# A four-layer hybrid on one core: the pacing estimate of TensorE, and where the first expert's products stand

## The chip, the core and the metric

The kernel runs on one core of a Trainium2 chip. The core has four compute engines, each with an instruction stream of its own that is worked off in order: TensorE (PE in the profile; its weight loads are PEld), VectorE (DVE), ScalarE (ACT) and GpSimd (POOL). SyncE (SP) issues the DMA transfers. The metric is the device time of one execution in microseconds, as a median over runs.

## What is computed

Four images of 32x32 positions (1024 tokens, 256 channels) go through four layers. Cut to what matters:

```python
# layer 0: norm, x @ w_in, 3x3 depthwise conv, gelu; then a selective scan with 512 channels, 64 states
dA = jnp.exp(dtt[:, :, None] * A)
h = dA * h + (dtt * xt)[:, :, None] * Bt[:, None, :]      # one step per token
y = jnp.einsum('bdn,bn->bd', h, Ct)
# layer 1: 1x1 conv, grouped 3x3 conv, 1x1 conv, relu
# layer 2: masked attention (8 heads of 32), then a mixture of 8 experts, hidden size 256
probs = softmax(tokens @ router_w.T); rw, re = top_k(probs, 2); rw = rw / rw.sum()
for e in range(8):
    h = gelu(tokens @ w1[e] + b1[e]); y = h @ w2[e] + b2[e]
    out = out + combine[:, e:e+1] * y
# layer 3: gated selective scan with 512 channels, 16 states; then 8 experts, hidden size 512
```

Each layer's output is added to its input or passed on. Every image needs, in this order: layer 0's front, the layer-0 scan, layers 1 and 2 and layer 3's front, the layer-3 scan, layer 3's end. The images don't depend on each other.

## The kernel before

**Scans.** A scan works in units of 128 rows (channels times states) by 1024 tokens: 256 units for an image in layer 0, 64 in layer 3, 1280 in all, in the order `SCANS` (L31): layer 0 of images 0 and 1, layer 3 of image 0, layer 0 of image 2, layer 3 of image 1, layer 0 of image 3, layer 3 of images 2 and 3. In the numbering of units used below, layer 3's scans begin at units 512, 832, 1152 and 1216. `scans` (L356) issues for each unit: a DMA that spreads the step sizes (`dA`), ScalarE's Exp, two bf16 products of 512 columns (`ps_rep`, L445), VectorE's multiply, VectorE's scan (`h`), GpSimd's multiply, and for every two units four fp32 products into 32 partitions each (`ps_y`, `pair`, L460).

**Side work.** Everything else is written as generators that yield between small steps. `STAGES` (L33) lists them: `front` (layer 0's start) of four images, `middle` (L1786: `back0`, `layer1`, `attention`, `moe(2)`, `front3`) of four, `last` (L1796: `back3`, `moe(3)`, store) of four. A `middle` may begin when its image's layer-0 scan is well on its way, a `last` likewise with layer 3. `advance` (L530) takes one step of the running stage, or chooses the next.

**The order.** Instructions of all engines go out in the order in which the Python code runs; no scheduler changes it. `run` (L552) interleaves by a clock per engine. A wrapper, `Metered`, adds an estimate in microseconds to the issuing engine's clock at every instruction; for TensorE the estimate is `matmul_us` (L71). Twice in each scan unit `run` does:

```python
now = clock["vector"]
for e in clock:
    clock[e] = max(clock[e], now - LAG)
for _ in range(TICKS):
    if max(clock.values()) > clock["vector"] + LEAD or self.advance() is None:
        break
```

So side work is handed out, at most two steps at a time, while no engine's clock is ahead of VectorE's. When all scan units are out, what is left of the stages follows without scans beside it.

**The forced path.** Five units before a scan whose inputs a side stage has not yet issued, `need` (L517) calls `advance` until they are, with no scan unit in between, and sets all clocks equal. `self.alone` then lets attention use the scan's PSUM banks (`ps_sx` for `ps_sc`).

**Attention.** `heads` (L1320) runs, for each of 8 blocks of 128 keys and each pair of heads, four fp32 and bf16 products into scores (`ps_sc`), two more bf16 ones for the mask, ScalarE's Exp, and four fp32 products into 32 partitions each (`ps_at`): 10 products a block, 640 an image.

**Experts.** `moe` (L1442) normalizes and transposes the tokens, makes the router's logits (`ps_lg`), then the routing: a chain of small VectorE operations (`route`, L1569), the transposes of the weights (`ps_ct`), the products with the second bias (`ps_b2`). After that the experts: a pipe of items, of which `one` issues TensorE's part, `two` the Gelu (`h_m`, ScalarE) or the weighted sum into `tb` (VectorE). An item "h" is 128 hidden channels of 512 tokens (two fp32 products of 512 columns, `ps_h`); an item "o" is 256 tokens of output (`ps_e`, fp32, 256 columns). `KH` is 2 in layer 2 and 4 in layer 3.

**Layer 3's front.** `front3` (L1624) makes `ps_p3` and `ps_g3`, the 512x512 product `ps_c3`, the states' inputs `ps_x3`, and in `steps` (L581) the step sizes `ps_dt` and their parts, which the scan needs.

Nearly every instruction goes through the wrapper, so the profile puts it on L124; groups are told apart by the names of their tiles. The profile leaves out digits that end a name (`ps_p` for `ps_p3`).

Of the kernel before, what the change touches and what calls it, by code (L numbers as in the profile page):

```python
# [7 lines left out]
F32 = mybir.dt.float32  # L8
BF16 = mybir.dt.bfloat16
I32 = mybir.dt.int32  # L10
AF = mybir.ActivationFunctionType
ALU = mybir.AluOpType
# [4 lines left out]
P = 128  # L17
NB = 4
L = 1024
TB = L // P  # L20
C = 256
# [3 lines left out]
NEXP = 8  # L25
# [38 lines left out]
def columns(x):  # L64
    n = 1
    for k in x.shape[1:]:
        n *= k
    return n


def matmul_us(out, lhsT=None, rhs=None, **_):  # L71
    if lhsT is None:
        lhsT = out
    us = 0.46e-3 * columns(out)
    if lhsT.dtype != BF16:
        us = max(4 * us, 0.3)
    if out.shape[0] <= 32:
        return us / 4
    return us / 2 if lhsT.shape[0] <= 32 else us


def by_columns(per, fixed, of=0):
# [9 lines left out]
class Metered:  # L92


    COST = {
        "tensor": {"matmul": matmul_us, "transpose": lambda out, *_: 0.3},
        "vector": {
            "tensor_tensor": by_columns(1.18, 0.06), "scalar_tensor_tensor": by_columns(1.5, 0.06),
# [34 lines left out]
class Hybrid:  # L133
# [1308 lines left out]
    def moe(self, which, b, tb):  # L1442

        nc, tc, a = self.nc, self.tc, self.a
        w1, w2, b1, hidden = (
            (a["L2_ffn_w1"], a["L2_ffn_w2"], self.vec["L2_ffn_b1"], 256) if which == 2
            else (a["L3_ffn_W1"], a["L3_ffn_W2"], self.vec["L3_ffn_b1"], 512)
        )
        KH = hidden // P
        with tc.tile_pool(name=f"m{which}{b}", bufs=1, side="right") as op:  # L1450
            xT = op.tile([P, 2, L], F32, name="xTm")
            cw = op.tile([P, TB, NEXP], F32, name="cw")

            def expert_weights(e):
                we1 = op.tile([P, 2, hidden], F32, tag="we1", name="we1", bufs=2)
                nc.sync.dma_start(we1, w1[e].rearrange("(k p) n -> p k n", p=P))
                we2 = op.tile([P, KH, C], F32, tag="we2", name="we2", bufs=2)
                nc.sync.dma_start(we2, w2[e].rearrange("(k p) n -> p k n", p=P))
                return we1, we2

            weights = {0: expert_weights(0)}
            with tc.tile_pool(name=f"mg{which}{b}", bufs=1, side="right") as gp:
                xn = gp.tile([P, TB, C], F32, name="xnm")
                yield from self.norm(gp, tb, TB, xn, "lnm")
                yield from self.turned(xn, TB, xT)
                lg = gp.tile([P, TB, NEXP], F32, name="lg")
                ps = self.ps("ps_lg", (P, TB, NEXP))
                for j in range(TB):
                    for k in range(2):
                        nc.tensor.matmul(  # L1470
                            ps[:, j, :], lhsT=xT[:, k, j * P : (j + 1) * P],
                            rhs=self.router[which][:, k, :], start=(k == 0), stop=(k == 1),
                        )
                yield 3.0
                if which == 2:
                    nc.vector.tensor_copy(lg, ps)
                else:
                    nc.vector.tensor_tensor(
                        lg, ps, self.gb.unsqueeze(1).to_broadcast([P, TB, NEXP]), ALU.add
                    )  # L1480
                yield 0.5
                if which == 2:
                    for j in range(0, TB, 2):
                        tj = tb[:, j : j + 2, :]
                        nc.gpsimd.tensor_tensor(tj, tj, xn[:, j : j + 2, :], ALU.add)
                        yield 0.6
                yield from self.route(gp, lg, cw, which == 2)

                cT = gp.tile([NEXP, L], F32, name="cT")

                def turn(g):
                    ps = self.ps("ps_ct")
                    for k in range(4):
                        nc.tensor.transpose(
                            ps[:NEXP, k * P : (k + 1) * P], cw[:, 4 * g + k, :], self.ident
                        )
                    nc.scalar.copy(cT[:, g * 512 : (g + 1) * 512], ps[:NEXP, :])

                yield from self.pipe(range(2), turn, cost=0.8)
                got = {}  # L1500

                def last(j):
                    got[j] = ps = self.ps("ps_b2", (P, 2, C))
                    for i in range(2):
                        m = 2 * j + i
                        nc.tensor.matmul(
                            ps[:, i, :], lhsT=cT[:, m * P : (m + 1) * P], rhs=self.b2[which],
                            start=True, stop=True,
                        )

                def add(j):
                    tj = tb[:, 2 * j : 2 * j + 2, :]
                    nc.vector.tensor_tensor(tj, got.pop(j), tj, ALU.add)

                yield from self.pipe(range(TB // 2), last, add, cost=1.0)

            hidden_of = {}
            got = {}

            def one(item):  # L1520
                kind, e, g, i = item
                we1, we2 = weights[e]
                if kind == "h":
                    if i == 0:
                        hidden_of[e, g] = op.tile([P, KH, 512], F32, tag="h", name="h_m", bufs=2)
                        if g == 1 and e + 1 < NEXP:
                            weights[e + 1] = expert_weights(e + 1)
                    got[item] = ps = self.ps("ps_h")
                    self.mm(
                        ps, lambda k: we1[:, k, i * P : (i + 1) * P], xT, 2,  # L1530
                        slice(g * 512, (g + 1) * 512),
                    )
                    return
                h = hidden_of[e, g]
                got[item] = ps = self.ps("ps_e", (P, 2, C))
                for s in range(2):
                    m = 2 * i + s
                    for f in range(KH):
                        nc.tensor.matmul(
                            ps[:, s, :], lhsT=h[:, f, m * P : (m + 1) * P], rhs=we2[:, f, :],  # L1540
                            start=(f == 0), stop=(f == KH - 1),
                        )

            def two(item):
                kind, e, g, i = item
                if kind == "h":
                    nc.scalar.activation(
                        hidden_of[e, g][:, i, :], got.pop(item), AF.Gelu,
                        bias=b1[:, e * KH + i : e * KH + i + 1],
                    )  # L1550
                    return
                ps = got.pop(item)
                for s in range(2):
                    m = 4 * g + 2 * i + s
                    nc.vector.scalar_tensor_tensor(
                        tb[:, m, :], ps[:, s, :], cw[:, m, e : e + 1], tb[:, m, :],
                        ALU.mult, ALU.add,
                    )

            items = []  # L1560
            blocks = [(e, g) for e in range(NEXP) for g in range(2)]
            for n in range(len(blocks) + 1):
                if n < len(blocks):
                    items += [("h", *blocks[n], i) for i in range(KH)]
                if n:
                    items += [("o", *blocks[n - 1], i) for i in range(2)]
            yield from self.pipe(items, one, two, cost=2.6 if which == 2 else 3.4)

    def route(self, gp, lg, cw, renorm):  # L1569

# [277 lines left out]
```

## Time and profile before

| | |
|---|---|
| median of 3 runs | 6643.48 us (6634.54 to 6644.86) |
| the profiled execution, its own time | 6636.95 us |
| its span, first to last instruction | 6635.2 us |
| TensorE busy / VectorE / GpSimd / ScalarE | 5360.8 / 5224.0 / 3653.8 / 3439.4 us |
| first scan begins, last scan ends | 204.4 us, 6196.8 us |
| longest stretch between two scans | 5494.2 to 5906.4 us (units 1211 and 1212) |
| mean granted clock of TensorE | 0.829 |

How to read it: the slices cut the span into 40 equal parts and give busy shares in tenths; the clock row is the granted TensorE clock in tenths. A group of instructions is told with its count, its busy time (overlaps counted once) and the mean of one. An fp32 product stands in the trace as two records, so counts of `x16` are eight products; the mean of a record includes its overlap with its neighbours. The rows that matter for what follows:

```profile
L124 POOL TENSOR_TENSOR h<-h,rows 128x1024 f32<-128x1024 f32 x1280 | 3033.0, 2372 | 1900.9 <-DVE h L124 1698.8
L124 DVE TENSOR_TENSOR_SCAN h<-dA,ps_rep 128x1024 f32<-128x1024 f32 x1280 | 2924.0, 2284 | 164.9 <-issue 25.2
L124 DVE TENSOR_TENSOR ps_rep<-ps_rep,rows 128x1024 f32<-128x1024 f32 x1280 | 1552.8, 1213 | 247.7 <-PE ps_rep L124 247.4
L124 PE MATMUL ps_rep<-S,spread_L_conv_A_log 96*128 96x512 bf16 x2048 | 767.5, 465 | 702.5 <-DVE h L124 674.3
L124 PE MATMUL ps_y<-h,collect_L_conv_A_log 128*32 128x512 f32 x4096 | 808.4, 767 | 77.5 <-POOL h L124 76.5
L124 PE MATMUL ps_h<-xTm,we 128*128 128x512 f32 x1536 | 718.9, 608 | 1.4 <-DVE tb L124 1.4
L124 PE MATMUL ps_e<-we,h_m 128*128 128x256 f32 x3072 | 699.6, 381 | 2.3 <-ACT h_m L124 2.3
```

### The profile page before, as it was taken

The page shows a single profiled execution, that of the slowest core. Times are in us where ns is not written, and L with a number is a line of the kernel's source. Part 1 is how long each engine was busy: PE and PEld are TensorE (multiplying, and loading weights), DVE is VectorE, ACT ScalarE, POOL GpSimd, SP SyncE. Part 2 cuts the span into 40 slices and gives each one's busy share as a digit, 9 for nine tenths or more (in the row PEclk, how much of TensorE's full clock was granted, in tenths as well). Part 3 has the DMA queues.
Part 4 walks back from the last instruction along what each step waited for, and adds up shares of the span by engine and source line. Part 5 has one row for each costly group of instructions (what it writes and reads, how often), then busy time and mean ns, then how long its engine had stood idle before and what let it go on. Part 6 is the DMA issues. An engine that isn't in the chain of part 4 may idle for free. (4 is left out here: it accounts for less than half of the span.)

```text
span 6635.2 us, 60077 instructions
## 1 busy us (share of the span) xinstructions
PE 5360.8 (81%) x20320; PEld 2159.1 (33%) x20320; DVE 5224.0 (79%) x4489; ACT 3439.4 (52%) x4114; POOL 3653.8 (55%) x1801
## 2 busy tenths in 40 slices
PE   6568778679798577979789779898699679878979
PEld 3003213122253022234235332243245222524656
DVE  8788998988798997789889997798999972248411
ACT  3426666445477334557658544477478344245411
POOL 0876786755557765555766665556856651045200
PEclk8558779589799568979879789989699789887989
DMA  2444554643245566335555664344644750146221
GB/s 74 151 153 157 182 171 163 190 139 124 101 153 170 190 168 155 112 116 172 175 165 168 189 166 133 105 139 169 200 154 161 196 148 21 45 131 169 74 64 35
DMA packets 348112, 936.90 MB, mean 141 GB/s; under 512 B 37140, under 2 KB 119648, under 8 KB 346144
## 3 DMA queue, kind: packets, MB, share of 16 engines
q1 hardware_dynamic: 345616, 930.35, 44.9%
q8 instruction: 172, 2.82, 0.2%
q0 software_dynamic: 2128, 2.13, 0.2%
q14 instruction: 196, 1.61, 0.1%
HBM read 842.59 MB, written 93.95 MB: 141 GB/s over the span
## 5 line engine op out<-in xcount | busy, mean ns | idle before, releaser
L124 POOL TENSOR_TENSOR h<-h,rows 128x1024 f32<-128x1024 f32 x1280 | 3033.0, 2372 | 1900.9 <-DVE h L124 1698.8
L124 DVE TENSOR_TENSOR_SCAN h<-dA,ps_rep 128x1024 f32<-128x1024 f32 x1280 | 2924.0, 2284 | 164.9 <-issue 25.2
L124 DVE TENSOR_TENSOR ps_rep<-ps_rep,rows 128x1024 f32<-128x1024 f32 x1280 | 1552.8, 1213 | 247.7 <-PE ps_rep L124 247.4
L124 ACT ACTIVATE dA<-dA,A_L_conv_A_log 128x1024 f32<-128x1024 f32 x1024 | 1148.6, 1145 | 609.6 <-DMA dA<-dt 528.6
L124 PE MATMUL ps_rep<-S,spread_L_conv_A_log 96*128 96x512 bf16 x2048 | 767.5, 465 | 702.5 <-DVE h L124 674.3
L124 PE MATMUL ps_y<-h,collect_L_conv_A_log 128*32 128x512 f32 x4096 | 808.4, 767 | 77.5 <-POOL h L124 76.5
L124 PE MATMUL ps_h<-xTm,we 128*128 128x512 f32 x1536 | 718.9, 608 | 1.4 <-DVE tb L124 1.4
L124 PE MATMUL ps_e<-we,h_m 128*128 128x256 f32 x3072 | 699.6, 381 | 2.3 <-ACT h_m L124 2.3
L124 ACT ACT_TABLE_LOAD x497 | 637.7, 1283 | 74.7 <-PE ps_h L124 41.7
L124 PEld LDWEIGHTS <-spread_L_conv_A_log 96*128 96x128 bf16 x2048 | 161.4, 103 | 1485.8 <-DVE h L124 1174.6
L124 PEld LDWEIGHTS ps_e<-we,h_m 128*128 128x128 f32 x3072 | 580.8, 190 | 146.8 <-issue 47.2
L124 DVE SCALAR_TENSOR_TENSOR tb<-ps_e,cw,tb 128x256 f32<-128x256 f32 x512 | 220.8, 474 | 411.1 <-PE ps_e L124 410.8
L124 ACT ACTIVATE h_m<-ps_h,cols 128x512 f32<-128x512 f32 x384 | 260.5, 687 | 485.9 <-PE ps_h L124 483.1
L124 ACT ACTIVATE p<-ps_sc 128x512 f32<-128x512 f32 x432 | 234.4, 594 | 474.7 <-PE ps_sc L124 464.8
L124 PEld LDWEIGHTS ps_h<-xTm,we 128*128 128x128 f32 x1536 | 292.9, 194 | 338.5 <-issue 294.0
L124 ACT ACTIVATE dA<-dA,A_L_attn_A_log 128x1024 f32<-128x1024 f32 x256 | 290.2, 1146 | 189.5 <-DMA dA<-dt 166.0
L124 PE MATMUL ps_at<-p,v 128*32 128x512 f32 x1024 | 354.8, 610 | 39.1 <-ACT p L124 28.2
L124 PE MATMUL ps_rep<-S,spread_L_attn_A_log 96*128 96x512 bf16 x512 | 184.9, 449 | 174.2 <-DVE h L124 163.3
L124 PE MATMUL ps_sc<-qT,kT 32*128 32x512 f32 x864 | 251.3, 653 | 30.1 <-issue 30.1
L124 PE MATMUL ps_at<-p,ones 128*32 128x512 f32 x1024 | 271.9, 610 | 0.0
L124 PEld LDWEIGHTS ps_y<-h,collect_L_conv_A_log 128*32 128x32 f32 x4096 | 107.6, 120 | 474.7 <-POOL h L124 226.9
L124 PE MATMUL ps_cv<-pad,diag 128*128 128x512 f32 x576 | 260.4, 594 | 0.0
(313 smaller groups left out, 5027.7 us busy)
## 6 DMA issues: line engine op xcount, KB each, us to landing
dA<-dt SPq DMA_DIRECT2D x1280, 512.0 KB
we<-in_L_ffn_W_dram SPq DMA_DIRECT2D x64, 512.0 KB
parts<-parts SPq DMA_DIRECT2D x64, 384.0 KB
S<-parts SPq DMA_DIRECT2D x96, 256.0 KB
dt<-sp_r SPq DMA_DIRECT2D x64, 256.0 KB
y<-yo SPq DMA_DIRECT2D x128, 128.0 KB
y_back<-y SPq DMA_DIRECT2D x64, 256.0 KB
we<-in_L_ffn_w_dram SPq DMA_DIRECT2D x64, 256.0 KB
```

Source lines behind the costliest of these rows:

```text
L124: return got(*args, **kw)
```

## The change

Two edits. First, `matmul_us` is written anew. The estimate of a product by its operands, before and after:

| product | before, us | after, us |
|---|---|---|
| bf16, 512 columns, more than 32 rows of weights (`ps_rep`, mask) | 0.236 | 0.369 |
| bf16, 512 columns, 32 rows | 0.118 | 0.230 |
| fp32, 512 columns, into 32 partitions or fewer (`ps_y`, `ps_at`) | 0.236 | 0.440 |
| fp32, 512 columns, 32 rows of weights (scores) | 0.471 | 0.653 |
| fp32, 512 columns, 128 rows (`ps_h`, convolutions) | 0.942 | 0.730 |
| fp32, 256 columns, 128 rows (`ps_e`) | 0.471 | 0.410 |
| fp32, 8 columns (`ps_lg`) | 0.300 | 0.400 |

Second, in `moe` the routing becomes a generator, and the pipe of expert items is made before it runs. After each of the routing's steps one step of the expert pipe is taken, up to 2 x KH of them (which are all "h" items, the first expert's hidden layer); the rest of the pipe runs after the routing. The functions inside (`turn`, `last`, `add`, `one`, `two`) only move. No instruction of the computation is added or removed; loads of ScalarE's tables, which are put in where needed, depend on the order.

```diff
 def matmul_us(out, lhsT=None, rhs=None, **_):
     if lhsT is None:
         lhsT = out
-    us = 0.46e-3 * columns(out)
-    if lhsT.dtype != BF16:
-        us = max(4 * us, 0.3)
-    if out.shape[0] <= 32:
-        return us / 4
-    return us / 2 if lhsT.shape[0] <= 32 else us
+    n = columns(out)
+    few = lhsT.shape[0] <= 32
+    if lhsT.dtype == BF16:
+        return (0.45e-3 if few else 0.72e-3) * n
+    if out.shape[0] <= 32 and n > 32:
+        return 0.86e-3 * n
+    return max(0.09 + (1.1e-3 if few else 1.25e-3) * n, 0.4)
...
-                yield 3.0
-                if which == 2:
+                def routing():
+                    yield 3.0
+                    if which == 2:
...
-                yield from self.route(gp, lg, cw, which == 2)
+                    yield from self.route(gp, lg, cw, which == 2)
...
-            yield from self.pipe(items, one, two, cost=2.6 if which == 2 else 3.4)
+                experts = self.pipe(items, one, two, cost=2.6 if which == 2 else 3.4)
+
+                ahead = 2 * KH
+                for cost in routing():
+                    yield cost
+                    if ahead:
+                        ahead -= 1
+                        yield next(experts)
+            yield from experts
```

More of the change, by code (lines that the diff above doesn't have):

```diff
@@ L1473, in moe @@
                         )
-                yield 3.0
-                if which == 2:
[L1476 to L1486, printed above, removed]
@@ L1487, in moe @@
-                yield from self.route(gp, lg, cw, which == 2)
[L1489 to L1495, printed above, removed]
-                        )
-                    nc.scalar.copy(cT[:, g * 512 : (g + 1) * 512], ps[:NEXP, :])
-                yield from self.pipe(range(2), turn, cost=0.8)
@@ L1500, in moe @@
-                got = {}
[L1502 to L1508, printed above, removed]
-                        )
-                def add(j):
-                    tj = tb[:, 2 * j : 2 * j + 2, :]
-                    nc.vector.tensor_tensor(tj, got.pop(j), tj, ALU.add)
@@ L1515, in moe @@
[L1515 to L1541, printed above, removed]
-                        )
@@ L1544, in two @@
[L1544 to L1566, printed above, removed]
-            yield from self.pipe(items, one, two, cost=2.6 if which == 2 else 3.4)
+                def routing():
+                    yield 3.0
+                    if which == 2:
+                        nc.vector.tensor_copy(lg, ps)
+                    else:
+                        nc.vector.tensor_tensor(
+                            lg, ps, self.gb.unsqueeze(1).to_broadcast([P, TB, NEXP]), ALU.add
+                        )
+                    yield 0.5
+                    if which == 2:
+                        for j in range(0, TB, 2):
+                            tj = tb[:, j : j + 2, :]
+                            nc.gpsimd.tensor_tensor(tj, tj, xn[:, j : j + 2, :], ALU.add)
+                            yield 0.6
+                    yield from self.route(gp, lg, cw, which == 2)
+                    cT = gp.tile([NEXP, L], F32, name="cT")
+                    def turn(g):
+                        ps = self.ps("ps_ct")
+                        for k in range(4):
+                            nc.tensor.transpose(
+                                ps[:NEXP, k * P : (k + 1) * P], cw[:, 4 * g + k, :], self.ident
+                            )
+                        nc.scalar.copy(cT[:, g * 512 : (g + 1) * 512], ps[:NEXP, :])
+                    yield from self.pipe(range(2), turn, cost=0.8)
+                    got = {}
+                    def last(j):
+                        got[j] = ps = self.ps("ps_b2", (P, 2, C))
+                        for i in range(2):
+                            m = 2 * j + i
+                            nc.tensor.matmul(
+                                ps[:, i, :], lhsT=cT[:, m * P : (m + 1) * P], rhs=self.b2[which],
+                                start=True, stop=True,
+                            )
+                    def add(j):
+                        tj = tb[:, 2 * j : 2 * j + 2, :]
+                        nc.vector.tensor_tensor(tj, got.pop(j), tj, ALU.add)
+                    yield from self.pipe(range(TB // 2), last, add, cost=1.0)
@@ new lines, in moe, with one @@
+                hidden_of = {}
+                got = {}
+                def one(item):
+                    kind, e, g, i = item
+                    we1, we2 = weights[e]
+                    if kind == "h":
+                        if i == 0:
+                            hidden_of[e, g] = op.tile([P, KH, 512], F32, tag="h", name="h_m", bufs=2)
+                            if g == 1 and e + 1 < NEXP:
+                                weights[e + 1] = expert_weights(e + 1)
+                        got[item] = ps = self.ps("ps_h")
+                        self.mm(
+                            ps, lambda k: we1[:, k, i * P : (i + 1) * P], xT, 2,
+                            slice(g * 512, (g + 1) * 512),
+                        )
+                        return
+                    h = hidden_of[e, g]
+                    got[item] = ps = self.ps("ps_e", (P, 2, C))
+                    for s in range(2):
+                        m = 2 * i + s
+                        for f in range(KH):
+                            nc.tensor.matmul(
+                                ps[:, s, :], lhsT=h[:, f, m * P : (m + 1) * P], rhs=we2[:, f, :],
+                                start=(f == 0), stop=(f == KH - 1),
+                            )
@@ new lines, in two @@
+                def two(item):
+                    kind, e, g, i = item
+                    if kind == "h":
+                        nc.scalar.activation(
+                            hidden_of[e, g][:, i, :], got.pop(item), AF.Gelu,
+                            bias=b1[:, e * KH + i : e * KH + i + 1],
+                        )
+                        return
+                    ps = got.pop(item)
+                    for s in range(2):
+                        m = 4 * g + 2 * i + s
+                        nc.vector.scalar_tensor_tensor(
+                            tb[:, m, :], ps[:, s, :], cw[:, m, e : e + 1], tb[:, m, :],
+                            ALU.mult, ALU.add,
+                        )
@@ new lines, in moe @@
+                items = []
+                blocks = [(e, g) for e in range(NEXP) for g in range(2)]
+                for n in range(len(blocks) + 1):
+                    if n < len(blocks):
+                        items += [("h", *blocks[n], i) for i in range(KH)]
+                    if n:
+                        items += [("o", *blocks[n - 1], i) for i in range(2)]
+                experts = self.pipe(items, one, two, cost=2.6 if which == 2 else 3.4)
[5 more added lines that the diff above has]
+                        yield next(experts)
```

## The prediction

> **What bounds the kernel now.** I read the slices first, to see where VectorE is idle, then the chain of waits to see what runs there, then windows cut at the starts of the scans.
>
> ```profile
> PE   6568778679798577979789779898699679878979
> DVE  8788998988798997789889997798999972248411
> PEclk8558779589799568979879789989699789887989
> ```
>
> VectorE carries the 1280 scan units (its columns are 166 us each) and is near full, except in slices 34 to 36 and in the last three. Its two instructions per unit, the multiply (1213 ns) and the scan (2284 ns), with the gaps between them come to 3.54 us in undisturbed stretches; 1280 units are then 4531 us of the 6635.2 us span. The rest is a start of 204 us, units that take longer than 3.54, one stall and a tail. The chain of waits names the stall's last third and the tail:
>
> ```profile
> 5802.61 14.45 PE ps_p L124 x32
> 5817.06 13.73 PE ps_g L124 x32
> 5830.79 27.47 PE ps_c L124 x64
> 5858.26 6.98 PE ps_x L124 x16
> ...
> 6314.23 13.83 PE ps_e L124 x64
> 6328.99 4.44 DMA out_dram<-tb
> ```
>
> No scan stands on it here: scan unit 1212 (image 3 of layer 3) cannot start before image 3's side work has made its inputs, and the last image's `last` stage cannot start before the last scans. The windows (columns: window, length, busy time and count of PE, weight loads, DVE, ACT, POOL, then granted clock, DMA share, GB/s):
>
> ```profile
> 2168.50:2390.50 222.00, 119.42 (x362) 14.29 (x360) 210.76 (x126) 76.17 (x73) 157.31 (x72) 0.52 0.58 186
> 1464.10:1746.70 282.60, 268.66 (x1396) 70.75 (x1394) 218.66 (x136) 147.31 (x215) 146.87 (x66) 0.97 0.34 115
> 512.60:620.00 107.40, 105.32 (x356) 38.84 (x354) 102.64 (x60) 71.86 (x91) 70.72 (x31) 1.00 0.49 168
> 3831.50:3929.80 98.30, 75.43 (x303) 38.90 (x303) 91.97 (x100) 41.14 (x53) 57.33 (x28) 0.83 0.62 155
> 5494.20:5641.20 147.00, 131.04 (x715) 35.77 (x712) 23.05 (x44) 58.74 (x73) 12.14 (x9) 0.96 0.05 15
> 5494.20:5906.40 412.20, 358.59 (x1391) 165.50 (x1388) 75.76 (x183) 150.87 (x212) 44.58 (x35) 0.92 0.12 38
> 5831.00:5906.40 75.40, 60.15 (x140) 24.19 (x138) 8.55 (x12) 39.74 (x58) 23.44 (x19) 0.95 0.22 61
> 6196.80:6328.00 131.20, 130.16 (x466) 87.00 (x464) 16.66 (x39) 25.82 (x37) 2.34 (x1) 1.00 0.08 27
> 6328.00:6635.20 307.20, 262.61 (x905) 176.74 (x904) 43.65 (x115) 53.34 (x82) 14.80 (x12) 0.89 0.17 53
> ```
>
> In order: 60 units with no side work (3.70 us each), 58 units with one image's attention (4.87 each, PE 95% busy), 30 units with convolutions (3.58 each, PE 98% busy), 22 units of layer 0's end and layer 1; the attention part of the stall, the whole stall, its end from the layer-3 convolution on; the rest of image 2's last experts, and image 3's `last` stage.
>
> **The change: the pacing.** The estimate sets no duration; it sets beside how many scan units a piece of side work is laid. By the formulas a scan unit costs TensorE 4 x 0.2355 = 0.94 us before and 2 x 0.369 + 2 x 0.440 = 1.62 after, against 3.55 on VectorE's clock, so side work gets 2.61 and then 1.93 us a unit. One key block of attention (10 products) costs 2.59 before and 4.27 after: 1.01, then 0.45 blocks a unit. The two programs' instruction order shows it: each image's 640 attention products stand beside 58 or 59 units before and 132 after; layer 2's experts beside 35 and then 39; layer 3's beside 81 in both. What then no longer fits has to go somewhere, and the order shows where, in three terms.
>
> *Tail.* Layer 3's `last` stages of images 0, 1 and (most of) 2 stood beside scans; now image 1's takes the place of image 2's beside the last 35 units, and images 2 and 3 both follow the last scan. Each whole stage is the 307.2 row; one more of it. The unfinished rest is 72 `ps_h` and 176 `ps_e` products after, 70 and 160 before; at 0.859 and 0.432 (6.87 us for 8 and 6.91 for 16 in the chain), +9. The new order of the first expert fills TensorE's pause in the routing, from the end of `ps_lg` at 6390.85 to `ps_ct` at 6396.35, 5.5 us a stage; its products are moved, not added, and its Gelu among the routing's Exp costs ScalarE one more table load of 1.28 us, on an idle engine. Twice -5.5. Tail: 307 + 9 - 11 = **+305**.
>
> *Stalls.* Layer 3's inputs for images 0 and 2 were ready 60 units before use. Now the scan's call for them finds them missing at units 508 and 1148: the order has 32 `ps_c3`, 8 `ps_x3`, the first `ps_dt`, and at 508 the last 11 of 16 `ps_g3`, at 1148 all 16 and 12 of 16 `ps_p3`, between two scans. From the convolution to the next scan took 75.4; `ps_g` is 13.73 for 16, `ps_p` 14.45 for 16. So 75.4 + 9.4 - 3.5 (a unit in flight) = 81, and 75.4 + 13.7 + 10.8 = 100. At 1212 image 3 has 80 of 640 products done where it had 240: 160 more at 147.0 / 400 = 0.37 are +59, less 5.5 of routing. Behind the scans' stall wait POOL's `h` multiply and the `ps_y` products, which nobody else needs then. Stalls: 81 + 100 + 54 = **+235**.
>
> *Units beside side work*, as time over 3.54 a unit. Attention before: 77, 74 and 74 in three images' windows and 21 in the fourth, 246. After, 401 units. No row shows attention this thin, so bounds: the convolutions' 3.58 with TensorE full below, 4.87 (nothing gained per unit) above. I take 3.70, the row without side work, since VectorE's own part of attention, 218.66 - 58 x 3.497 = 16 us over 132 units, gives 3.66 already: 64 over, so -182. Layer 2's experts: 152.3, 154.2 and 153.2 for 35 units are 88 over; by TensorE's work (150.5 + 4 x 1.1 for four more units, at 98%) 157.5 for 39, 58 over: -30. One `last` fewer beside scans: its expert units -27 (316.4 for 81 is 30 over), its start of 13 units -28 (3349.1 to 3423.1 for unit 720 to 733). The convolution and step units now inside the stalls: -30. Sum **-297**. The 1.1 is TensorE's part of one warm scan unit: 105.32 less 84 products at 0.859, by 30.
>
> Total 305 + 235 - 297 = +243 on the profiled execution's 6636.95 (span and 1.75 around it): 6880. The median of the runs is 6.5 higher; I leave that inside the range.
>
> **A rule against the row.** TensorE's granted clock lies between half and full: the scan-only row has 0.52, attention 0.97, and the row with PE 77% busy 0.83. Thin attention needs 4.85 products of 0.32 us ((268.66 - 58 x 1.1) / 640) and 1.1 a unit, 2.65 of 3.70, 72%: by the rows mostly warm, and at 0.8 still 3.3, under 3.70. The Trainium skill (TensorE: Matmul & The Clock Gate, "HAM oscillation — how this bites in real kernels") says that an idle gap over about 3.4 us drops the array to half speed; it speaks against thinning dense work. By it, if such gaps came at every block, attention would run cold and the sum would be the cold rival's; by the row it isn't.
>
> **The rivals.**
> - *Cold clock.* Thin attention drops to the half clock and TensorE binds it: 1.99 a unit for the scan (119.42 / 60) and 4.85 x 0.64 = 3.10 are 5.09 against 3.70; 396 units, +550: 7430, and half of it 7155. For: scan-only units run at 0.52. Against: at 5.09 TensorE is full, which is where the rows are warm. 9%.
> - *The scans gain more than the tail loses, faster.* One mechanism: with TensorE's queue shorter at all times, every unit comes near the scan-only pace. Units beside side work took 5581 (6196.8 - 204.4 less the stall) and take 5284 in my sum, 4.13 each; the kernel breaks even at 5041, 3.94 each, and at 3.70 throughout would take 6880 - 548 = 6330. For: VectorE waited 247 us for `ps_rep`. Against: scan-only units beside scatters or at a change of scan take 4.16 to 4.29, and the layer-0 end 4.5 with TensorE a quarter idle. 5%.
> - *The two new stalls cost little*, their chain hidden by queued units: 6880 - 181 = 6700. Against: the old one showed its chain in full. 6%.
> - *The estimate does not match the durations it is named after*: 0.73 for a 512-column product that takes 0.859, so experts would be overfed. But they already run at 98% and go from 35 to 39 units; it changes nothing by itself and is in the sum.
>
> **How the numbers follow.** My forecast has 78%, with 6780 to 6990 by its own bounds: attention at 3.54 (-64) with cheaper stalls (-36) below, attention at 3.98 (+110) above. To leave out no more than 2 in 10 the range takes part of the two neighbours: 6750 to 7030. Faster than 6630 (0.2%, what can be told from no change) only by the second rival and some of the 2% unnamed: 5%; within 0.2%: 2%; slower: 93%.
>
> **What would show it.** A span near 6880; after the last scan some 740 us with two `ps_o3` groups; gaps between scans near 81 and 100 us at units 508 and 1148 and of 466 at 1212; attention units at 3.6 to 3.9 with the clock above 0.75; TensorE's pause in the routing gone. Wrong, if attention's clock is near 0.5, if the units average under 3.94, or if a gap is missing.

## The result and the profile after

The changed kernel takes 6910.23 us (median of 4 runs, 6902.81 to 6916.29), the kernel before on the same chip 6640.8 us. The ratio is 1.0408, 95% interval 1.0395 to 1.0421: slower by 4%, 30 us above the forecast and inside its range. The profiled execution's span is 6912.9 us, 277.7 more than before.

The busy tenths in 40 slices (173 us each now):

```profile
PE   6568768678869777787978987886877889698989
DVE  8789999989989598998998998998949321871111
PEclk9558769688879877887978988887977989698989
```

VectorE now has four columns of 1 at the end instead of the two, and two new dents (a 5 in slice 14, a 4 in slice 30). Those are the two new gaps and the longer tail. The windows cut there (window, length, busy time and count of PE, weight loads, DVE, ACT, POOL, granted clock, DMA share, GB/s): image 0's attention, the gaps between scans at units 507, 1147 and 1211 (so the units that wait are 508, 1148 and 1212), and after the last scan the rest of image 1's experts and the `last` stages of images 2 and 3.

```profile
1492.80:1988.10 495.30, 401.63 (x1838) 85.88 (x1836) 468.59 (x285) 224.99 (x290) 321.43 (x140) 0.83 0.47 147
...
2284.30:2363.70 79.40, 71.88 (x169) 28.71 (x167) 9.61 (x11) 40.85 (x59) 23.18 (x18) 0.98 0.21 68
5037.10:5132.20 95.10, 87.58 (x205) 35.65 (x203) 9.61 (x11) 46.67 (x67) 21.90 (x17) 0.98 0.15 52
...
5419.30:5884.30 465.00, 415.43 (x1668) 179.14 (x1664) 77.91 (x182) 167.99 (x229) 43.18 (x34) 0.93 0.09 30
```

```profile
6180.70:6318.90 138.20, 136.41 (x488) 91.27 (x486) 18.34 (x44) 26.60 (x38) 2.34 (x1) 1.00 0.10 33
6318.90:6613.30 294.40, 259.88 (x904) 175.21 (x904) 42.75 (x114) 56.91 (x85) 14.80 (x12) 0.91 0.17 52
6613.30:6912.90 299.60, 260.85 (x904) 175.84 (x904) 43.65 (x115) 55.59 (x84) 14.80 (x12) 0.91 0.18 55
```

In the gaps and in the tail TensorE is busy and VectorE is not: the same work as before, without scans beside it. Beside thin attention (laid beside 132 units instead of 58) it is the other way: VectorE is busy 468.59 of 495.30 us, and a unit takes 3.75 us instead of 4.87. Term by term, from the spans of the two profiled executions:

| term | predicted, us | measured, us | how measured |
|---|---|---|---|
| start | 0 | +2.9 | first scan at 207.3 instead of 204.4 |
| gaps at 507, 1147, 1211 | +235 | +227 | 79.4 + 95.1 + 465.0, less 412.2 |
| units beside side work | -297 | -246 | 5333.9 (6180.7 - 207.3 - 639.5) instead of 5580.2 |
| tail | +305 | +294 | 732.2 instead of 438.4 |
| sum | +243 | +278 | 6912.9 - 6635.2 |

### The profile page after: what moved, and what is told of

Same layout as the page of the kernel before. It is cut to its first block, busy times and chain, and to the rows that moved or that the text cites. A ratio compares the mean times of both kernels' runs of the same rounds, so it can differ in the third digit from the quotient of the medians.

```text
span 6912.9 us, 59875 instructions
## 1 busy us (share of the span) xinstructions
PE 5463.7 (79%) x20320; PEld 2153.0 (31%) x20320; DVE 5217.5 (75%) x4489; ACT 3251.6 (47%) x3959; POOL 3650.0 (53%) x1801
## 5 line engine op out<-in xcount | busy, mean ns | idle before, releaser
L125 DVE TENSOR_TENSOR ps_rep<-ps_rep,rows 128x1024 f32<-128x1024 f32 x1280 | 1549.8, 1211 | 98.7 <-PE ps_rep L125 97.8
L125 PE MATMUL ps_y<-h,collect_L_conv_A_log 128*32 128x512 f32 x4096 | 785.9, 759 | 82.6 <-POOL h L125 82.4
L125 ACT ACTIVATE p<-ps_sc 128x512 f32<-128x512 f32 x400 | 217.1, 594 | 792.1 <-PE ps_sc L125 792.0
L125 PE MATMUL ps_at<-p,ones 128*32 128x512 f32 x1024 | 320.4, 709 | 0.0
L125 PE MATMUL ps_sc<-qT,kT 32*128 32x512 f32 x800 | 276.6, 765 | 29.6 <-issue 28.3
L125 POOL TENSOR_TENSOR sp_l<-sp_l,sp_e 128x512 f32<-128x512 f32 x64 | 81.1, 1267 | 376.0 <-DVE sp_e L125 340.4
```

What stands on the lines that cost most here:

```text
L125: return got(*args, **kw)
```

## Experiments

The theory: the estimate moves work, in the order, to where no scan runs beside it; neither thin attention nor the moved products cost much themselves. The rivals: the new order inside the expert stage is a good part of the loss; or thin attention is.

**The two edits apart.** `est_only` is the kernel before with the new `matmul_us`; `order_only` is the changed kernel with the old one.

```diff
 # order_only, against the changed kernel
-    n = columns(out)
...
+    us = 0.46e-3 * columns(out)
+    if lhsT.dtype != BF16:
+        us = max(4 * us, 0.3)
+    if out.shape[0] <= 32:
+        return us / 4
+    return us / 2 if lhsT.shape[0] <= 32 else us
```

> The new estimate with the old order inside the expert stage. Theory (the estimate alone lays side work thinner, so layer 3's inputs miss their scans at units 508 and 1148 and a second last stage falls behind the scans): the instruction order has the same two gaps and the same tail, so 6910 plus one routing pause of 5.5 us for each exposed expert stage (one in the stall at 1212, two in the tail) plus some 9 us for 16 transposes and 4 more products in the gap at 1148: 6930, between 6900 and 6945. Rival (the first expert's products between the routing's steps hold VectorE up, as its waits of 2 to 3 us for the second bias's products suggest, and are a good part of the loss): 6870 or less.

Measured: 6937.36 us, ratio to the kernel before 1.0447 (1.0429 to 1.0464). The gaps (windows of this kernel; the last is its tail):

```profile
2281.00:2362.10 81.10, 73.59 (x173) 29.46 (x171) 9.62 (x11) 39.22 (x58) 23.16 (x18) 0.98 0.19 66
5031.40:5133.80 102.40, 94.85 (x227) 39.54 (x227) 9.61 (x11) 52.24 (x78) 23.12 (x18) 0.96 0.18 62
5425.60:5889.60 464.00, 414.06 (x1653) 179.60 (x1664) 77.84 (x182) 165.40 (x227) 43.13 (x34) 0.92 0.09 30
6186.00:6937.20 751.20, 664.15 (x2311) 448.27 (x2310) 104.79 (x270) 135.26 (x204) 31.96 (x25) 0.91 0.16 48
```

The estimate alone makes the whole loss; the first rival falls. The second edit is a gain of 27 us on top of it, 19 of them in the tail (751.2 against 732.2) and 9 in the two new gaps. In the big gap it gains nothing: 464.0 without it, 465.0 with it. VectorE does wait longer for the second bias's products with the new order (59.0 us against 37.7), but the units beside side work take the same 5334 us in both.

> The old estimate with the new order inside the expert stage. Theory: only the two exposed routing pauses are filled, 2 x 5.5 us: 6630 against 6641, between 6615 and 6645. Rival (the moved products delay the scans in the five covered expert stages): above 6660.

Measured: 6649.25 us, 1.0012 (1.0003 to 1.0022): a miss, between both. With the old estimate the new order makes the kernel no faster. The big gap is 418.3 us instead of 412.2; the tail is 423.5 instead of 438.4; the units beside side work take 5607 us instead of 5580. The profiled execution was the slowest of its ten (6659.02 us, median 6649.25), so some 10 of these 27 us may be its own.

Why the big gap gains nothing stands in its chain of waits. First without the new order (`est_only`), then with it (the changed kernel); columns are start, length, what ran:

```profile
5643.27 6.64 PE ps_lg L125 x32
...
5656.17 1.87 PE ps_ct L125 x8
5658.03 7.12 PE ps_b L125 x16
5665.15 9.84 PE ps_h L125 x16
5674.99 3.45 PE ps_e L125 x16
```

```profile
5635.49 6.63 PE ps_lg L125 x32
5642.12 8.09 PE ps_h L125 x12
5650.23 0.69 ACT h_m L125
5650.94 1.28 ACT L125
5652.23 0.27 ACT lg L125
...
5657.69 1.88 PE ps_ct L125 x8
5660.22 7.19 PE ps_b L125 x16
5667.41 5.72 PE ps_e L125 x16
```

The routing's Exp (`ACT lg`) stands behind Gelus (`ACT h_m`) of the first expert in ScalarE's queue, and the last of these waits for its products and is followed by a table load. So the Exp begins 10.1 us after the end of `ps_lg` (5652.23). TensorE has only four items to do ahead in layer 2; they end at 5651.9, before the late routing does, and it pauses for 5.8 us, where it paused for 6.3 in the kernel before and in `est_only` (the number in brackets is TensorE's idle time before `ps_ct`, first before, then after):

```profile
5667.56 1.86 PE L124 MATMUL ps_ct<-ident,cw 128*8 128x128 f32 x8 [6.27 <-DVE cw L124]
```

```profile
5657.69 1.86 PE L125 MATMUL ps_ct<-ident,cw 128*8 128x128 f32 x8 [5.78 <-DVE cw L125]
```

From the end of `ps_lg` to the first `ps_e` it is 25.1 us without and 25.3 with the new order. In layer 3 there are eight items to do ahead; TensorE works on them until `ps_ct` can start (14.2 us after `ps_lg`), and the tail gains.

**The price that does it.** Of the new prices, `into32_old` puts back the one for fp32 products into 32 partitions; `into32_058` sets it between; `y_old` puts it back for the scans' own collecting products only.

```diff
     if out.shape[0] <= 32 and n > 32:
-        return 0.86e-3 * n
+        return 0.46e-3 * n        # into32_old; 0.58e-3 in into32_058
```

> The changed kernel, with the price of fp32 products into 32 partitions (attention's values and sums, and the scans' own collecting products) put back from 0.440 to 0.236 us for 512 columns; the other new prices stay. Theory: this one price makes attention thin and the images late. The order has no gap at 508 or 1148 and one last stage behind the scans; attention stands beside 86 units, 479 of its products are left in the stall where the kernel before had 419 (+22 us at 0.37), the rest after the scans is 11 us shorter, two routing pauses are 11 shorter, units beside attention gain some 100 and those beside the experts (27 and 66 units instead of 35 and 81) lose as much: 6640, between 6590 and 6690. Rival (the loss comes from the prices of the wide fp32 products, or from TensorE's clock beside thin attention wherever it stands): 6780 or more.

Measured: 6632.84 us, 0.9986 (0.9976 to 0.9996). That one price carries the loss: without it no input is late at 508 or 1148 and one `last` stage follows the scans. Its big gap and its tail:

```profile
5476.70:5910.60 433.90, 384.22 (x1464) 172.85 (x1468) 77.79 (x183) 153.89 (x218) 43.29 (x34) 0.91 0.10 33
6215.40:6629.60 414.20, 374.61 (x1332) 250.59 (x1328) 59.26 (x151) 79.37 (x118) 17.16 (x13) 0.94 0.16 48
```

For the gap the terms of the expectation make 412 + 22 - 5.5 = 429.

> As the run with that price put back, but at 0.297 us for 512 columns (0.58 ns a column), between old and new. The order still has no gap at 508 or 1148 and one last stage behind the scans, but attention is laid wider. Theory (wider attention gains in the scans as long as no input is late): 30 us less than the kernel before, 6610, between 6570 and 6650. Rival (thin attention itself costs): slower than the run with the price put back by 20 us or more.

Measured: 6647.2 us, 1.0008 (0.9998 to 1.0018): a miss. The units beside side work took 5539 us and not 5577 as in `into32_old`, a gain of 38 as expected in kind, but the big gap grew from 433.9 to 489.8 us, since less of image 3's attention was done by unit 1212. The input at 1212 is late in every kernel here, and the expectation had left that out.

> The changed kernel with only the scans' own collecting products (ps_y) put back to 0.236 us; attention's products into 32 partitions keep the new 0.440. The order: attention beside 109 units, no gap at 508 or 1148, one last stage behind the scans, but all 640 attention products of image 3 in the stall at 1212 (560 were there in the changed kernel, 479 with both put back). Theory (late inputs cost, thin attention does not): the stall some 30 us longer than the changed kernel's 465, the other two gaps (174 us) and the second last stage (293 us) gone, the units beside side work 240 us longer since that stage is among them again: 6690, between 6650 and 6730. Rival (thin attention itself costs): 6800 or more.

```diff
             h = [state.pop(k - 1), state.pop(k)]
+            INTO32[0] = 0.46e-3        # matmul_us returns INTO32[0] * n
             for g in range(2):
...
+            INTO32[0] = 0.86e-3
             if i == per - 1:
```

Measured: 6687.77 us, 1.0064 (1.0050 to 1.0078). Its attention, gap and tail:

```profile
1470.30:1876.20 405.90, 324.47 (x1647) 76.70 (x1665) 390.40 (x239) 197.63 (x263) 267.35 (x117) 0.92 0.46 147
5455.00:5965.90 510.90, 453.88 (x1816) 197.03 (x1831) 80.23 (x191) 186.89 (x251) 52.95 (x42) 0.92 0.10 32
6272.40:6690.90 418.50, 379.45 (x1332) 254.72 (x1328) 59.33 (x152) 79.33 (x118) 17.14 (x13) 0.93 0.15 47
```

Attention is almost as thin as in the changed kernel (109 units at 3.72 us), with one `last` stage in the tail, and the kernel is 222 us faster than the changed one. Thin attention is not what costs; the second rival falls. And most of the loss hangs on a price that is not attention's at all: that of the scans' own `ps_y`, which is taken off in every unit and so leaves less room for all side work. The rest of the price into 32 partitions, attention's, makes 55 us more (6687.77 less 6632.84): the gap at 1212 grows by 77 (510.9 against 433.9), and the units beside side work gain 23.

**The routing's Exp first.** Products are taken only after the step that issues it.

```diff
-                for cost in routing():
+                for n, cost in enumerate(routing()):
                     yield cost
-                    if ahead:
+                    if ahead and n >= (6 if which == 2 else 2):
```

> The changed kernel with the same postponement. Theory: 5.5 us from the pause in the stall, some 4 from three products fewer in the gaps at 508 and 1148 each, some 5 to 10 from the covered stages: 6893 against 6910, between 6878 and 6903. Rival: 6907 or more.

Measured: 6892.79 us, 1.0380 (1.0366 to 1.0394), as the theory had it.

> The old estimate and the new order, but the first expert's products are taken only after the routing's Exp has been issued. Theory (ScalarE works in order: with a Gelu of the first expert ahead of the routing's Exp, the whole routing waits for that expert's products, so TensorE's pause is moved and not filled in the stall, and beside the scans VectorE's adds of the second bias come later): the stall at 1212 falls from 418 to 412 us or less, the covered expert stages lose the 6 to 14 us each that they took longer in the run with the new order alone, and the time falls from 6649 to 6628, between 6610 and 6640. Rival (the products themselves, not the Gelu, hold the routing up): 6643 or more, the stall still at 418.

Measured: 6646.38 us, 1.0008 (0.9999 to 1.0017): a miss in the time. The big gap did fall, from 418.3 to 407.4 us, and in the changed kernel from 465.0 to 453.4. That is about twice the pause of 5.8. The chain in `order_late`:

```profile
5678.00 6.63 PE ps_lg L124 x32
5684.63 9.75 PE ps_h L124 x16
5694.38 0.45 PE ps_ct L124 x4
...
5695.95 3.71 PE ps_b L124 x16
5699.67 5.34 PE ps_e L124 x16
```

No pause before `ps_ct`, and `ps_b` takes 3.71 us where it took 7.19 with the new order alone. What the run did not give back is the time beside scans: 5612 us, still some 30 over the kernel before, with or without the postponement. The trace places it: layer 2's routing and experts beside scans took 735 us for three images, against 704 before, and in the whole kernel VectorE waited twice as long for `ps_b`, whose products now come after the first expert's (first in the kernel before, then in `order_late`: us in total, times, longest):

```profile
DVE tb L124 <- PE ps_b L124: 30.1, 16, 4.1
```

```profile
DVE tb L124 <- PE ps_b L124: 60.5, 20, 10.7
```

Another cause fits as well: the order shows the five covered expert stages ending two to four units earlier, and a unit laid beside nothing hides 2.4 us of TensorE less (3.54 less 1.1). No run tested either alone, so the cause of these 30 us stays open.

> The run with the price for 32 partitions put back, with the same postponement. Theory: 5.5 us from the stall and some 10 from the covered stages: 6617 against 6633, between 6600 and 6628, faster than the kernel before by 0.2% or more. Rival: 6630 or more.

Measured: 6622.87 us, 0.9970 (0.9958 to 0.9982), its big gap 424.2 us instead of 433.9: faster than both kernels, 0.3% below the one before.

**The wide product at its duration.** In the trace eight fp32 products of 512 columns take 6.87 us back to back, 0.859 each; the new estimate has 0.730.

```diff
 # wide_086, against into32_old_late; wide_081 has 1.4e-3 and the old 0.46e-3
-        return 0.46e-3 * n
-    return max(0.09 + (1.1e-3 if few else 1.25e-3) * n, 0.4)
+        return 0.4e-3 * n
+    return max(0.09 + (1.1e-3 if few else 1.5e-3) * n, 0.4)
```

> The run with the postponed products and the old price for 32 partitions, with the wide fp32 product priced as the trace has it back to back (0.858 us for 512 columns instead of 0.730) and the products into 32 partitions at 0.205 us. The order: experts of layer 2 beside 34 units instead of 27, attention beside 82, no gap at 508 or 1148, one last stage behind the scans, but all 640 attention products of image 3 in the stall at 1212 instead of 479 (+60 us at 0.37). Theory (work is cheapest where it just keeps TensorE full beside the scans; each unit more for a stage that fills TensorE hides 2.4 us of it): the experts' units gain more than the stall loses, 6590, between 6555 and 6618. Rival (what is gained beside the scans comes back in the stall, as with 0.297 us): 6623 or more.

Measured: 6571.85 us, 0.9903 (0.9888 to 0.9918), the fastest here. Attention, layer 2's experts (33 units), and the big gap:

```profile
1465.00:1775.00 310.00, 272.28 (x1493) 70.22 (x1512) 297.53 (x185) 169.12 (x235) 202.63 (x89) 1.00 0.44 146
1859.20:2006.60 147.40, 141.09 (x571) 78.59 (x569) 138.64 (x137) 116.64 (x109) 77.96 (x33) 0.98 0.42 140
5363.90:5838.10 474.20, 422.93 (x1716) 179.89 (x1732) 77.89 (x182) 169.89 (x228) 51.77 (x42) 0.92 0.10 31
```

82 units of attention already run at 3.78 us each, close to the 3.75 of 132; more units buy nothing. The experts take 4.47 us a unit, against 4.98 over the 27 units in `into32_old_late`:

```profile
1898.40:2032.80 134.40, 133.62 (x535) 76.80 (x533) 118.70 (x121) 103.87 (x98) 63.75 (x27) 0.99 0.41 131
```

The gap is 50 us longer than there, and the scans gain more than that.

> As the run before it, with the wide product at 0.807 us and the products into 32 partitions at the old 0.236: the same deadlines met, layer 2's experts beside 32 units, all 640 products in the stall. Theory: between the two, 6600, from 6570 to 6620. Rival: 6623 or more.

Measured: 6604.14 us, 0.9944 (0.9931 to 0.9958), between the two. It has the same price into 32 partitions as `into32_old_late`, so the wide price alone is worth 17 us there (0.9970 less 0.9944 of 6640; by the two intervals some 12 us either way); the step on to `wide_086` mixes two prices.

## Why the prediction was right, and where it was off

- *Gaps.* 81, 100 and 466 us forecast, 79.4, 95.1 and 465.0 measured. The counts came from the instruction order, the prices from the same work standing alone in the trace before. The third agrees in part by chance. Its attention part grew by 56 us (147.0 before, 202.7 now, 5419.3 to 5622.0) where +59 stood. The routing's pause, which was to give 5.5, gave nothing: the sum took layer 3's 5.5 for layer 2's 6.3, and counted the Gelu among the routing's Exp as one table load on an idle engine, where the Gelus held the Exp up for 10.1 us. And the end from `ps_dt` to the next scan came out 6 us shorter (5849.2 to 5884.3, against 5865.2 to 5906.4), which no term had.
- *Tail.* One more stage, as forecast, and +7.0 for the unfinished rest (138.2 less 131.2) where +9 stood. The two stages took 294.4 and 299.6 us where the row had 307.2. The pause in the routing was worth 9 us and not 5.5: from the end of `ps_lg` to the end of the last `ps_e` it is 238.0 us before (6390.85 to 6628.83) and 229.0 and 229.3 after (6384.28 to 6613.27, 6677.17 to 6906.49). The half clock behind the pause goes with it: `ps_b` took 7.12 us there before and 3.65 after.
- *Attention.* 3.70 a unit forecast, 3.73 to 3.75 measured; 3.70 was the row without side work. The gain was 160 us (246 less 86 over 3.54 a unit) instead of 182.
- *Experts beside scans, the term that was mis-sized most.* "Layer 2's experts beside 35 and then 39" counted six units of the routing as units of the experts. Without them it is 33 (units 462 to 495). Routing and experts together took 233 to 237 us in 48 units before and 247 to 250 in 50 after: +22 for three images, over 3.54 a unit, where -30 stood in the sum. In `est_only` the same stretches are +18, so most of it is the estimate's.
- *The covered term as a whole* was 51 us too favourable, and that is in part luck: 52 by the experts and 22 by attention, less 23, since the other three terms (-27, -28 and -30) came to -108 together and not to -85. What made these 23 was not taken apart.
- *Rivals.* The cold clock did not come: attention ran at a granted clock of 0.82 to 0.85 with PE busy 81% (401.63 of 495.30). The scans did gain on the whole, to 4.17 us a unit (5333.9 / 1280) and not to the 3.94 that would have broken even. Both new gaps showed in full.
- *"It changes nothing by itself"*, of the wide product's price of 0.73, does not hold with the old price into 32 partitions: priced nearer its duration it brought 17 us (`wide_081`) and, together with a lower price into 32 partitions, 44 (`wide_086`, 0.9970 less 0.9903). In the changed kernel itself it was not run alone.

Image 0's routing and experts beside scans, first in the kernel before (48 units), then in the changed one (50 units); the other two images are within some 4 us of these:

```profile
1746.70:1983.80 237.10, 196.63 (x758) 103.66 (x758) 209.63 (x230) 150.16 (x155) 124.32 (x57) 0.83 0.38 129
```

```profile
1988.10:2235.10 247.00, 198.74 (x770) 103.18 (x770) 217.57 (x232) 152.11 (x157) 128.90 (x59) 0.83 0.39 126
```

## What to carry to other kernels

An estimate that paces an order is not right because it is like the durations: it decides who runs beside whom, and what it delays has to be followed to its deadline and to the tail. Count in the built order which work ends up with nothing beside it, and price that from the rows where the same work already stands alone. When independent work is moved into a pause, look at every queue it enters: here Gelus in front of the Exp moved the pause instead of filling it.

## What the runs showed of the hardware

The half clock appeared in a place the prediction had not looked at, after the routing's pause. Granted clock of TensorE (the third number from the end) from `ps_ct` to the end of `ps_b`, first in the kernel before (layer 3, after a pause of 5.5 us), then of `ps_b` alone in `order_late` (layer 2, no pause before `ps_ct`):

```profile
6396.20:6405.30 9.10, 8.95 (x25) 6.07 (x25) 2.08 (x4) 2.43 (x3) 0.00 (x0) 0.50 0.00 0
```

```profile
5695.90:5699.70 3.80, 3.75 (x17) 2.98 (x17) 2.07 (x3) 0.58 (x2) 0.00 (x0) 1.00 0.18 61
```

The same 16 records take 7.12 us at 0.50 and 3.71 at 1.00. The Trainium skill (TensorE: Matmul & The Clock Gate, "Why this matters for your kernels") asks for no gap above about 3 us between bursts; the pause of 5.5 us and its price agree with that. Attention that leaves TensorE idle a fifth of the time (busy 401.63 of 495.30 us) had a mean clock of 0.83, below the 0.97 of the dense attention before but far from one half.
